# A graph-attention kernel: two more blocks of x through the main loop, and another order of the drain

## The chip, the cores and the metric

The kernel runs on one core of one Trainium2 chip. The metric is the time of one execution on the device in microseconds; of several executions the median is taken. The core has a matrix engine (TensorE, PE in the profile, its weight loads PEld), VectorE (DVE), ScalarE (ACT), GpSimd (POOL), and SyncE (SP), which here only issues DMAs. Sixteen DMA engines carry all transfers.

## The reference, cut to what matters

```python
# x (4096, 512), adj (4096, 4096), W (512, 4*512), a (4, 1024, 1), all float32
ht  = (x @ W).reshape(N, 4, 512).transpose(1, 0, 2)         # four heads
src = einsum('hnd,hd->hn', ht, a[:, :512, 0])
dst = einsum('hnd,hd->hn', ht, a[:, 512:, 0])
e   = leaky_relu(src[:, :, None] + dst[:, None, :], 0.01) + adj[None]
att = softmax(e, axis=-1)
x   = layernorm(x + einsum('hij,hjd->hid', att, ht).mean(axis=0))
```

The entries of adj are 0 or random numbers up to 1e9, and are added to the scores. Where the largest entry of a row leads the second by more than the scores can differ, the softmax is 1 in that column and 0 elsewhere, and the row's result is the layer norm of x[row] + x[col] @ mean of the heads of W.

## The kernel before

`leading_rows` computes that short form for all rows and counts the rows where the lead is too small; `general` would do the whole softmax for blocks that have such rows, behind a branch on the count, and does not run with these inputs. The 4096 rows make NB = 32 blocks of 128; partition p of block ib is row 32 p + ib, so several blocks of x next to each other are one longer run per partition.

For one block the steps are these. VectorE takes maxima of the 64 segments of 64 columns (`segment_maxima`), then the largest segment and its index (`find_segment`). GpSimd gathers that segment of each row from adj in HBM (`lead`, by an indirect DMA). VectorE finds the place in it, and GpSimd gathers the rows x[col] (`find_column`, tile `y`). PE transposes y and ScalarE copies it out of PSUM (`turn`, tile `yt`). `products` multiplies it, in four steps of 128 columns, with the mean of the heads of W (`w_sum`), and `residual` adds the block's x to the same sum by a product with the identity. ScalarE makes the statistics from the sum (`stats`), GpSimd the root (`rstd`), ScalarE the normalised block (`finish`), into the tile `hold`, in which x lay. `row_norm` makes the sums of squares of x for the test.

The main loop runs over t from 0 to 31; in step t the block t is searched, block t − 2 gathers (`COLUMN`), t − 3 is multiplied (`PROJECT`), t − 4 has its statistics (`STATS`) and each second step a pair t − 6 and t − 5 is finished (`FINISH`). The order of all work on each engine is the order of the program text (`manual_schedule`).

All loads and stores of adj, x and out stand on one queue, SP's, in the order of the text. A block of adj is 2 MB; it is loaded whole, or in four pieces of 512 KB for block 0 and the last four (`LATE` = 28 and on), five blocks ahead (`AHEAD`). The x of blocks 0 to 23 comes between the blocks of adj, four blocks at a time (`x_at`). The last eight blocks (`BEHIND` = 24 and on) have their x loaded behind all of adj, two blocks at a time, in step 31. Blocks 24 to 27 are therefore multiplied without x; ScalarE puts their sum by (`put_by`, line 234), and once x is there GpSimd adds it for 24 to 26 and VectorE for 27 (`add_x`, line 237). Block 28 takes its residual at the head of step 31.

After the loop comes the drain: the stores of the finished blocks are issued, blocks 29, 30 and 31 are gathered, transposed and multiplied, the leftover blocks normalised, the bound for the test made (`bound`, in parts), the test and its count done (`test`, `count`, `report`), and the last stores issued. Blocks 28 to 31 and 27 have their statistics and normalisation from VectorE (`moments`, `factor`, `normalise`) with the root on ScalarE; block 31 is multiplied and normalised in two halves. Block 31's column is searched in the whole row of adj (`find_column_in_row`, line 201) rather than in a gathered segment.

Of the kernel before, what the change touches and what calls it, by code (L numbers as in the profile page):

```python
# [9 lines left out]
F32 = mybir.dt.float32  # L10
# [10 lines left out]
P = 128  # L21
# [45 lines left out]
def leading_rows(ctx, tc, x, adj, W, a, out, ident, v, n_bad, any_bad):  # L67
# [15 lines left out]
    LATE = NB - Q  # L83
    BEHIND = LATE - Q

# [126 lines left out]
    def residual(ib):  # L212
        o_ps[ib] = psum.tile([P, D], F32, name="o")
        nc.tensor.matmul(o_ps[ib], ident, hold[:, ib, :], start=True, stop=False)  # L214

# [140 lines left out]
    def bound(part):  # L356

        if part == 0:
            xm = once.tile([P, 1], F32, name="xm")
            nc.vector.tensor_reduce(xm, xx, axis=AX.X, op=OP.max)  # L360
            px = of_bound[0] = psum.tile([1, P], F32, name="px", bufs=1)
            nc.tensor.transpose(px, xm, ident)
        elif part == 1:
            nc.vector.tensor_reduce(xg, of_bound[0], axis=AX.X, op=OP.max)
            nc.scalar.activation(xg, xg, AF.Sqrt)
            pb = of_bound[1] = psum.tile([P, 1], F32, name="px", bufs=1)
            nc.tensor.matmul(pb, ones[0:1, :], xg, start=True, stop=True)
        else:
            nc.vector.tensor_mul(lead_by, of_bound[1], vn)
            nc.vector.tensor_scalar(lead_by, lead_by, 1.05, 110.0, op0=OP.mult, op1=OP.add)  # L370
# [23 lines left out]

    x_at = {lo - 1: (lo, Q) for lo in range(Q, BEHIND, Q)}
    vectors = [(kb, h) for kb in range(KB) for h in range(H)]
# [3 lines left out]
    for t in range(NB):  # L400
# [13 lines left out]
        if t == NB - 1:  # L414
            for ib in (BEHIND, LATE, BEHIND + 2, LATE + 2):
                load_x(ib, 2)
            row_norm(BEHIND)
            row_norm(BEHIND + 1)
            add_x(nc.gpsimd, BEHIND)
        find_segment(t)  # L420
# [11 lines left out]
        if ib >= 0:  # L432
            turn(ib)
            if ib > BEHIND:
                products(ib - 1, KB - 1, KB)
            if ib < BEHIND or ib == LATE:
                residual(ib)
# [12 lines left out]

    row_norm(BEHIND + 2)
    row_norm(BEHIND + 3)
    row_norm(LATE)
    store(nc.sync, 0, Q)
    for ib in range(Q, BEHIND, 2):
        store(nc.sync, ib, 2)
    find_column(NB - 2)
    add_x(nc.gpsimd, BEHIND + 1)
    find_column_in_row(NB - 1)
    add_x(nc.gpsimd, BEHIND + 2)  # L460
    turn(NB - 3)
    products(NB - 4, KB - 1, KB)
    residual(NB - 3)
    products(NB - 3)
    for ib in range(LATE + 1, NB):
        row_norm(ib)
    stats(BEHIND)
    moments(LATE)
    bound(0)
    for ib in range(BEHIND, NB):  # L470
        find_inner(ib)
    factor(LATE)
    normalise(LATE, o_ps.pop(LATE))
    turn(NB - 2)
    residual_in_halves(NB - 1)
    products(NB - 2, 0, 1)
    bound(1)
    add_x(nc.vector, LATE - 1)
    stats(BEHIND + 1)
    moments(LATE - 1)  # L480
    products(NB - 2, 1, KB - 1)
    rstd(slice(BEHIND, BEHIND + 2))
    stats(BEHIND + 2)
    bound(2)
    test()
    pg = count()
    rstd(slice(BEHIND + 2, BEHIND + 3))
    moments(NB - 3)
    factor(LATE - 1, shift=True)
    report(pg)  # L490
    factor(NB - 3)
    normalise(NB - 3, o_ps.pop(NB - 3))
    turn(NB - 1)
    finish(BEHIND)
# [9 lines left out]
    normalise(NB - 2, o_ps.pop(NB - 2))  # L504
    finish(BEHIND + 2)
    finish(BEHIND + 3)
    stats_of_half(NB - 1, 1)
    moments(NB - 1)
    factor(NB - 1, shift=True)
    finish_in_halves(NB - 1)  # L510
    for ib, n in ((NB - 4, 1), (NB - 3, 1), (BEHIND, 2), (NB - 2, 1), (BEHIND + 2, 2)):
        store(nc.sync, ib, n)
# [154 lines left out]
```

## Time and profile before

| | |
|---|---|
| median of 6 runs | 242.54 us (242.29 to 243.21) |
| the profiled execution | 242.08 us, span 240.5 us |
| busy: PE, DVE, ACT, POOL | 83%, 78%, 46%, 42% of the span |
| DMA | 97.73 MB, mean 406 GB/s |
| adj on the SP queue | 27 transfers of 2 MB, 20 of 512 KB |
| x on the SP queue | 6 of 1 MB, 4 of 512 KB |
| stores | 1 of 1 MB, 12 of 512 KB, 4 of 256 KB |

Times in the profile are from the start of the span; the span leaves some 1.6 us of the execution's time outside. In a row of the timeline stand the start, the time taken, the engine, the line, the operation with its tiles and shapes, how many instructions are taken together, and in brackets the engine's idle time before and what ended it. A tile is named as in the program (`seg<-adj_t`: written and read). A 128x512 product in float32 shows as two instructions, so four steps of `products` are eight. The DMA share is the mean busy share of the sixteen engines; it can pass 1 slightly, as packets overlap.

### The profile page before, as it was taken

How to read it: one execution, taken by the hardware profiler on the slowest of the kernel's cores; microseconds unless marked ns; L12 is line 12 of the kernel's file. 1: busy time of each engine (PE TensorE's matmuls, PEld its weight loads, DVE VectorE, ACT ScalarE, POOL GpSimd, SP SyncE). 2: the span in 40 equal slices, each digit the busy share in tenths (PEclk: the TensorE clock that was granted, in tenths of full speed). 3: DMA queues.
4: the chain of work that ended last, by engine and by line, in shares of the span. 5: the costliest groups of instructions: out<-in, count | busy, mean ns of one | idle time of the engine just before them, and what ended most of it. 6: DMA issues, size and time to landing. Idle time of an engine off the chain costs nothing.

```text
span 240.5 us, 2519 instructions
## 1 busy us (share of the span) xinstructions
PE 199.5 (83%) x683; PEld 102.6 (43%) x683; DVE 187.0 (78%) x308; ACT 111.8 (46%) x267; POOL 101.3 (42%) x215
## 2 busy tenths in 40 slices
PE   0198959999999899999959978599878869698990
PEld 0135515656666566655424433143433423243560
DVE  2635784489869985999589969987799999897781
ACT  2002002155757566564635554446464645156771
POOL 1102322316426452646352753454365565567210
PEclk9999778999999999999997999979999999999998
DMA  6999999999999999999999999999999999999995
GB/s 241 440 417 422 420 431 406 425 422 405 424 426 419 403 424 422 415 411 431 403 428 422 411 420 419 418 410 418 415 424 399 399 400 405 396 411 416 418 401 217
DMA packets 14849, 97.73 MB, mean 406 GB/s; under 512 B 2280, under 2 KB 2280, under 8 KB 9968
## 3 DMA queue, kind: packets, MB, share of 16 engines
q1 hardware_dynamic: 11232, 88.09, 89.0%
q0 software_dynamic: 3584, 9.44, 10.1%
q8 instruction: 6, 0.10, 0.2%
q14 instruction: 11, 0.09, 0.1%
q10 hardware_dynamic: 16, 0.02, 0.0%
HBM read 89.15 MB, written 8.39 MB: 405 GB/s over the span
## 4 chain that ended last, share of the span: by engine, by line
issue 34%; POOL 30%; DMA 22%; PE 7%; DVE 3%; ACT 1%; POOLq 1%; SPq 1%
DMA adj_t<-in_adj_dram 15%; POOL lead L171 10%; POOL y L181 9%; DMA y<-in_x_dram,col 7%; PE o L221 3%; POOL sd L249 3%; POOL start L176 2%; POOL col L195 2%; POOL row L169 2%; DVE seg L158 2%; PE o L263 1%; PE tp L208 1%; POOL sd L248 1%; POOL nm L250 1%; SPq L113 1%
## 5 line engine op out<-in xcount | busy, mean ns | idle before, releaser
L158 DVE TENSOR_REDUCE seg<-adj_t 128x32 f32<-128x2048 f32 (+1 forms) x74 | 146.3, 1987 | 38.9 <-DMA adj_t<-in_adj_dram 38.1
L221 PE MATMUL o<-w_sum,yt 128*128 128x512 f32 x248 | 116.5, 610 | 0.7 <-ACT yt L210 0.7
L221 PEld LDWEIGHTS o<-w_sum,yt 128*128 128x128 f32 x248 | 45.5, 194 | 54.5 <-issue 44.1
L210 ACT COPY yt<-tp 128x512 f32<-128x512 f32 x32 | 18.8, 587 | 46.6 <-PE tp L208 46.6
L171 POOL DMA_INDIRECT lead<-in_adj_dram,row x32 | 32.3, 1010 | 14.1 <-POOL row L169 14.1
L181 POOL DMA_INDIRECT y<-in_x_dram,col x32 | 30.9, 965 | 16.1 <-POOL col L195 15.1
L311 PE MATMUL o<-hold,ident 128*128 128x512 f32 x32 | 21.0, 818 | 14.9 <-DMA hold<-in_L_gnn_W_dram 14.9
L208 PE MATMUL tp<-ident,y 128*128 128x128 f32 x128 | 20.0, 280 | 15.4 <-DMA y<-in_x_dram,col 15.3
L214 PE MATMUL o<-hold,ident 128*128 128x512 f32 x52 | 28.0, 620 | 0.2 <-DMA hold<-in_x_dram 0.2
L208 PEld LDWEIGHTS tp<-ident,y 128*128 128x128 f32 x128 | 14.4, 142 | 28.7 <-issue 27.0
L195 POOL TENSOR_TENSOR col<-start,within 128x1 uint32<-128x1 uint32 x31 | 5.9, 190 | 48.7 <-DVE within L193 48.6
L329 ACT COPY wt<-tp 128x512 f32<-128x512 f32 x16 | 9.2, 587 | 31.5 <-PE tp L327 26.9
L169 POOL TENSOR_TENSOR row<-at,first 128x1 uint32<-128x1 uint32 x32 | 6.1, 190 | 38.6 <-DVE at L167 38.6
L228 ACT ACTIVATE sq<-hold 128x512 f32<-128x512 f32 x32 | 19.8, 619 | 2.9 <-DMA hold<-in_x_dram 2.9
L335 PEld LDWEIGHTS pv<-at_d,wt 128*128 128x128 f32 x128 | 16.3, 191 | 6.8 <-ACT wt L329 3.5
L311 PEld LDWEIGHTS o<-hold,ident 128*128 128x128 f32 x32 | 8.1, 264 | 25.4 <-POOL row L169 10.9
L312 ACT ACTIVATE w_sum<-o 128x512 f32<-128x512 f32 x4 | 2.4, 598 | 33.4 <-PE o L311 33.4
L254 ACT ACTIVATE hold<-o,nm,sd 128x512 f32<-128x512 f32 x24 | 17.2, 771 | 0.0
L245 ACT ACTIVATE sq<-o,nm 128x512 f32<-128x512 f32 x24 | 16.5, 688 | 0.8
L335 PE MATMUL pv<-at_d,wt 128*128 128x2 f32 x128 | 15.3, 244 | 0.6 <-ACT wt L329 0.6
L243 ACT ACTIVATE sq<-o 128x512 f32<-128x512 f32 x24 | 14.6, 608 | 0.0
L327 PEld LDWEIGHTS tp<-ident,hold 128*128 128x128 f32 x64 | 7.9, 142 | 6.9 <-issue 6.9
(85 smaller groups left out, 137.6 us busy)
## 6 DMA issues: line engine op xcount, KB each, us to landing
adj_t<-in_adj_dram SPq DMA_DIRECT2D x27, 2048.0 KB
adj_t<-in_adj_dram SPq DMA_DIRECT2D x20, 512.0 KB
hold<-in_x_dram SPq DMA_DIRECT2D x6, 1024.0 KB
out_dram<-hold SPq DMA_DIRECT2D x12, 512.0 KB
hold<-in_L_gnn_W_dram SPq DMA_DIRECT2D x4, 1024.0 KB
hold<-in_x_dram SPq DMA_DIRECT2D x4, 512.0 KB
out_dram<-hold SPq DMA_DIRECT2D x1, 1024.0 KB
out_dram<-hold SPq DMA_DIRECT2D x4, 256.0 KB
```

The source lines that it names most:

```text
L158: nc.vector.tensor_reduce(seg_of[ib][:, ts(k, S // n)], adj_t[ib][:, ts(k, N // n)].rearrange("p (s e) -> p s e", e=E), axis=AX.X, op=OP.max,)
L171: nc.gpsimd.indirect_dma_start(out=lead, out_offset=None, in_=adj_segs, in_offset=bass.IndirectOffsetOnAxis(ap=row[:, :1], axis=0),)
L181: nc.gpsimd.indirect_dma_start(out=y, out_offset=None, in_=x, in_offset=bass.IndirectOffsetOnAxis(ap=col[:, :1], axis=0),)
L208: nc.tensor.transpose(tp[:, kb, :], y[:, ts(kb, P)], ident)
L210: nc.scalar.copy(yt, tp)
L214: nc.tensor.matmul(o_ps[ib], ident, hold[:, ib, :], start=True, stop=False)
L221: nc.tensor.matmul(o_ps[ib], yt_of[ib][:, kb, :], w_sum[:, kb, :], start=(start and kb == 0), stop=(kb == KB - 1),)
L228: nc.scalar.activation(sq, hold[:, ib, :], AF.Square, accum_out=xx[:, ib : ib + 1])
L245: nc.scalar.activation(sq, o, AF.Square, bias=nm[:, i], accum_out=sd[:, i])
L254: nc.scalar.activation(hold[:, ib, :], o_ps.pop(ib), AF.Identity, bias=nm[:, i], scale=sd[:, i])
L311: nc.tensor.matmul(o, ident, hold[:, w_at + kb * H + h, :], start=(h == 0), stop=(h == H - 1))
L335: nc.tensor.matmul(pv[:, kb, h : 2 * H : H], wt[:, k, :], at_d[:, k, h : 2 * H : H], start=(k == 0), stop=(k == KB - 1),)
```

## The change

`BEHIND` goes from 24 to 26. The x of blocks 24 and 25 is one more load between the blocks of adj, issued in step 23 ahead of adj block 28, so the loads behind adj become three (blocks 28 and 29, then 26 and 27, then 30 and 31) instead of four. Blocks 24 and 25 then go the loop's usual way, with residual on PE, statistics in steps 28 and 29 and finish in step 30; only 26 and 27 are put by, and GpSimd adds x for 26 and VectorE for 27. Block 28 is multiplied in step 31 without its residual, which comes after the loop with its last product. In the drain the sums of squares, the inner maxima, the parts of the bound (four now), the test's count and `turn` of block 31 stand elsewhere, block 27's and 29's moments are apart, and a pair fewer is finished.

```diff
-    BEHIND = LATE - Q
+    BEHIND = LATE - 2
     def residual(ib):
-        o_ps[ib] = psum.tile([P, D], F32, name="o")
-        nc.tensor.matmul(o_ps[ib], ident, hold[:, ib, :], start=True, stop=False)
+        start = ib not in o_ps
+        if start:
+            o_ps[ib] = psum.tile([P, D], F32, name="o")
+        nc.tensor.matmul(o_ps[ib], ident, hold[:, ib, :], start=start, stop=False)
 ...
             nc.scalar.activation(xg, xg, AF.Sqrt)
-            pb = of_bound[1] = psum.tile([P, 1], F32, name="px", bufs=1)
+        elif part == 2:
+            pb = of_bound[2] = psum.tile([P, 1], F32, name="px", bufs=1)
             nc.tensor.matmul(pb, ones[0:1, :], xg, start=True, stop=True)
 ...
-    x_at = {lo - 1: (lo, Q) for lo in range(Q, BEHIND, Q)}
+    x_at = {lo - 1: (lo, min(Q, BEHIND - lo)) for lo in range(Q, BEHIND, Q)}
 ...
         if t == NB - 1:
-            for ib in (BEHIND, LATE, BEHIND + 2, LATE + 2):
+            for ib in (LATE, BEHIND, LATE + 2):
                 load_x(ib, 2)
-            row_norm(BEHIND)
-            row_norm(BEHIND + 1)
-            add_x(nc.gpsimd, BEHIND)
 ...
-            if ib < BEHIND or ib == LATE:
+            if ib < BEHIND:
                 residual(ib)
 ...
-    row_norm(BEHIND + 2)
-    row_norm(BEHIND + 3)
-    row_norm(LATE)
+    for ib in range(BEHIND, LATE + 2):
+        row_norm(ib)
     store(nc.sync, 0, Q)
     for ib in range(Q, BEHIND, 2):
         store(nc.sync, ib, 2)
     find_column(NB - 2)
-    add_x(nc.gpsimd, BEHIND + 1)
+    add_x(nc.gpsimd, BEHIND)
     find_column_in_row(NB - 1)
-    add_x(nc.gpsimd, BEHIND + 2)
+    residual(LATE)
+    products(LATE, KB - 1, KB)
     turn(NB - 3)
-    products(NB - 4, KB - 1, KB)
     residual(NB - 3)
-    products(NB - 3)
-    for ib in range(LATE + 1, NB):
-        row_norm(ib)
-    stats(BEHIND)
+    products(NB - 3, 0, KB - 1)
+    row_norm(NB - 2)
+    row_norm(NB - 1)
     moments(LATE)
-    bound(0)
     for ib in range(BEHIND, NB):
         find_inner(ib)
+    bound(0)
+    products(NB - 3, KB - 1, KB)
+    stats(BEHIND)
     factor(LATE)
     normalise(LATE, o_ps.pop(LATE))
+    bound(1)
     turn(NB - 2)
     residual_in_halves(NB - 1)
-    products(NB - 2, 0, 1)
-    bound(1)
+    bound(2)
     add_x(nc.vector, LATE - 1)
-    stats(BEHIND + 1)
     moments(LATE - 1)
-    products(NB - 2, 1, KB - 1)
-    rstd(slice(BEHIND, BEHIND + 2))
-    stats(BEHIND + 2)
-    bound(2)
+    products(NB - 2, 0, 2)
+    bound(3)
     test()
     pg = count()
-    rstd(slice(BEHIND + 2, BEHIND + 3))
+    products(NB - 2, 2, KB - 1)
+    rstd(slice(BEHIND, BEHIND + 1))
+    report(pg)
+    turn(NB - 1)
     moments(NB - 3)
     factor(LATE - 1, shift=True)
-    report(pg)
     factor(NB - 3)
     normalise(NB - 3, o_ps.pop(NB - 3))
-    turn(NB - 1)
     finish(BEHIND)
     finish(BEHIND + 1)
 ...
-    finish(BEHIND + 2)
-    finish(BEHIND + 3)
 ...
-    for ib, n in ((NB - 4, 1), (NB - 3, 1), (BEHIND, 2), (NB - 2, 1), (BEHIND + 2, 2)):
+    for ib, n in ((NB - 4, 1), (NB - 3, 1), (BEHIND, 2), (NB - 2, 1)):
         store(nc.sync, ib, n)
```

More of the change, by code (lines that the diff above doesn't have):

```diff
@@ L365, in bound @@
             nc.scalar.activation(xg, xg, AF.Sqrt)
-            pb = of_bound[1] = psum.tile([P, 1], F32, name="px", bufs=1)
+        elif part == 2:
+            pb = of_bound[2] = psum.tile([P, 1], F32, name="px", bufs=1)
             nc.tensor.matmul(pb, ones[0:1, :], xg, start=True, stop=True)
         else:
-            nc.vector.tensor_mul(lead_by, of_bound[1], vn)
+            nc.vector.tensor_mul(lead_by, of_bound[2], vn)
             nc.vector.tensor_scalar(lead_by, lead_by, 1.05, 110.0, op0=OP.mult, op1=OP.add)
```

## The prediction

> **What bounds the kernel now.** I read the page's slices first. The DMA row says that the sixteen DMA engines are full from the second slice to the last but one, while PE is not.
>
> ```profile
> PE   0198959999999899999959978599878869698990
> DVE  2635784489869985999589969987799999897781
> DMA  6999999999999999999999999999999999999995
> ...
> HBM read 89.15 MB, written 8.39 MB: 405 GB/s over the span
> ```
>
> 97.5 MB at the 415 or so GB/s of the middle slices is 235 us of a 240.5 us span: the kernel moves bytes, and computing matters only where it leaves an engine of the DMA without work. So the second view is the table by windows over the last microseconds (columns: window, its length, busy time of PE, PEld, DVE, ACT and POOL, granted clock, DMA share, GB/s).
>
> ```profile
> 236.25:236.50 0.25, 0.00 (x0) 0.00 (x0) 0.00 (x0) 0.00 (x0) 0.00 (x0) 1.00 0.74 295
> ...
> 236.75:237.00 0.25, 0.00 (x0) 0.00 (x0) 0.00 (x0) 0.00 (x0) 0.00 (x0) 1.00 0.59 238
> 237.00:237.25 0.25, 0.00 (x0) 0.00 (x0) 0.00 (x0) 0.00 (x0) 0.00 (x0) 1.00 1.03 401
> ...
> 238.00:238.25 0.25, 0.00 (x0) 0.00 (x0) 0.00 (x0) 0.00 (x0) 0.00 (x0) 1.00 0.28 115
> ...
> 238.75:239.00 0.25, 0.00 (x0) 0.00 (x0) 0.00 (x0) 0.00 (x0) 0.00 (x0) 0.50 0.17 66
> ```
>
> The second figure from the right is the one to read. The last store (block 31, 256 KB) is issued at 236.16. Before it, between 236.25 and 237.0, a quarter to two fifths of the engines have nothing to do; at 237.0 it reaches them and all are busy. But the last to end, at 239.0, are two or three of sixteen (0.17). 256 KB is 16 KB for each engine, 0.63 us at 415/16 = 26 GB/s; an engine that ends at 239.0 began that store only at about 238.35, 1.35 us after it had reached the idle ones. Those late engines were not waiting for it: they had older stores to finish. This decides the forecast.
>
> The third view is the SP queue in its single issues, with what each waited for, beside the reduces of VectorE.
>
> ```profile
> 211.39 0.33 SPq L306 DMA_DIRECT2D out_dram<-hold  x1
> SPq L306 <- DMA adj_t<-in_adj_dram: 1.4, 1, 1.4
> ...
> 212.85 0.33 SPq L306 DMA_DIRECT2D out_dram<-hold  x1
> SPq L306 <- DMA hold<-in_x_dram: 1.1, 1, 1.1
> ...
> 210.48 3.45 DVE L158 TENSOR_REDUCE seg<-adj_t 128x16 f32<-128x1024 f32 x3
> ```
>
> After the last adj piece (issued 198.95) come four loads of x and then the stores. The four x loads and the first four stores wait for pieces of adj, the next four stores for the x loads: a transfer is issued when the eighth before it has landed. So the issue times tell landings: block 30's four pieces at 200.27, 202.27, 203.50 and 204.95, block 31's at 206.94, 208.17, 209.60 and 211.39, the first x load at 212.85. VectorE takes the pieces of block 31 at 208.49, 210.48, 211.63 and 212.78 (3.45 us is three of 1.15): it is 0.7 to 1.6 us behind the stream there.
>
> Last, the tail, from the timeline of PE and DVE.
>
> ```profile
> 219.09 1.02 PE L221 MATMUL o<-w_sum,yt 128*128 128x512 f32 x2
> ...
> 232.94 0.55 DVE L290 TENSOR_SCALAR hold<-hold,mv,sd 128x512 f32<-128x512 f32 x1
> ...
> 234.14 0.43 DVE L297 BATCH_NORM_STATS2 halves_st<-o 128x6 f32<-128x256 f32 x1 [0.65 <-PE o L263]
> ```
>
> From block 29's transposes (218.62, when its y has landed) PE works nearly without a pause to 234.11. The first row is block 28's last product, behind them; the last is block 31's second half of statistics, for which VectorE waited 0.65 us on PE. Root, normalise and the last store follow.
>
> **The change part by part.**
>
> *x of blocks 24 and 25 (512 KB) moves ahead of the sixteen pieces of blocks 28 to 31.* Bytes, number and size of transfers stay as they were, the stores too (one of 1 MB, twelve of 512 KB, four of 256 KB before and after), so each DMA engine has the same work. Each piece takes the place of the transfer after it: block 30 lands at 202.27, 203.50, 204.95 and 206.94 against uses at 203.14, 204.46, 205.61 and 206.76; block 31 at 208.17, 209.60, 211.39 and 212.85 against 208.49, 210.48, 211.63 and 212.78. Two are late, by 0.18 and 0.07. VectorE has 0.58 us of waiting for the lead gather just before 210.27, which swallows the first. Cost: 0.1 us. Without that cover, if VectorE kept up with the stream, it would be the whole place, 1.4 us. In steps 24 to 27 x comes long before its use. The other x loads land where they did (block 28 about 214.1, blocks 26 and 27 about 215.5).
>
> *Blocks 24 and 25 in the loop.* PE gets two residuals of 0.86 us (two passes of 0.43) in steps 27 and 28. It waited for y 1.47 us before block 25's transposes (197.51), 0.54 before block 26's and 1.88 before block 27's (208.22): covered; without that each would cost 0.86. ACT gets statistics and square sums there (0.60 + 0.69 + 0.62 plus reads, some 2.1 us per block) and loses two copies of 0.59; its gaps before the next yt copy are 3.0, 1.9 and 4.6 us: covered. POOL gets the three rstd operations (1.2 us) in step 30, between y of block 28 (ends 206.57) and the row of block 30, which comes at 208.66: covered. POOL loses two additions of 1.27 us; the one in step 31 held block 31's row by 0.25 us, the other ended before y of block 31, which VectorE's search of a whole row (215.13 to 219.55) releases. So the gathers of y stand as they were, but for 0.2 us at block 30. The finish of both blocks goes to step 30, and their store becomes the twelfth on SP, ahead of block 28's, waiting for nothing but the queue.
>
> *The drain's order on PE.* Block 28 needs its residual no more at the head of step 31, where PE and PEld waited 0.2 and 1.0 us for x, and ACT's yt copy comes 1 us earlier without the two square sums ahead of it. From 212.43: transposes 0.63, block 27's last product 0.86, three of block 28 2.58, residual and last product 1.72, end at 218.2, before y of block 29 lands at 218.5. So 0.86 us leaves the stretch behind 218.62, which PE then ends at 233.25 instead of 234.11. VectorE follows only in part: the root for block 29 now stands on ACT behind the copy of block 31 (228.2 transposes, 228.9 copy, 229.5 root, 229.9 normalise, as now 229.94), so its chain up to the normalise of block 30 still ends at 232.94 + 0.55 = 233.49, and only then comes the second half of block 31. That is 234.14 − 233.49 = 0.65 us gained; bounds 0 (a count or root that waits longer; the test's matmul now stands between products) and 0.86 (VectorE as quick as PE). The last store leaves SP at 235.5.
>
> *What this is worth at the end.* Bounds: 0.65 us if the last store is what ends last, 0 if the loaded engines do. The trace is nearest to 0: the engines that ended at 239.0 had work until 238.35. An issue reaches free engines about 0.85 us later (236.16 to 237.0), so the last store could come as late as 237.5 without moving the end. I take 0.2 us, for small gaps in the late engines' queues that a store waiting earlier would fill. [...]
>
> Sum: 0.2 us off the profiled run's 242.08, that is 241.9; this run was 0.46 under the median 242.54, so 242.3.
>
> **The rivals.**
>
> *Faster: the late engines are late by accident.* Most engines end at 238.2, two or three at 239.0. If their lag (0.75 us) is not there in the new program, the earlier store counts too: −0.65 to −0.95, 241.6 to 241.9. For it: something must have set these few back, and code loading uses the same engines (two instruction queues, 17 packets; six of them take 0.2% of 16 × 240.5 us, 1.3 us each), so its place can move. Against: the code is nearly as long.
>
> *Slower, by the DMA: one such load more, or one on an engine already late.* Place: the last 12 us. Price: 1.3 − 0.2 = +1.1 us, or about half if it falls on an engine less late, 243.0 to 243.6. It decides once an engine with no spare time gets it in the drain. Against: as above.
>
> *Slower, by the stream: adj late on VectorE.* All pieces of blocks 30 and 31 now land within 0.1 to 1.0 us of their use. If the place costs its full 1.4 us, the last store goes at 236.9: still before 237.5, so no change. From a delay of 2.0 us it counts one to one; 2.5 us gives 243.0. Little speaks for that.
>
> *No effect to measure:* this is the forecast itself.
>
> **How the numbers follow.** Forecast, within 0.2% (0.49 us, about what a measurement can tell from no change): 0.53, its own range 242.1 to 242.7. Late engines gone: 0.27. One load more: 0.13; the stream: 0.07. So faster 0.27, same 0.53, slower 0.20. The range leaves one in ten on either side: 241.6 (the faster rival's far end) to 243.1 (into the slower rivals).
>
> **What would show it.** Right: VectorE's last reduce of block 31 still at 212.8 to 212.9; last product of block 28 ahead of block 29's transposes; last store issued about 235.5; DMA share 1.0 from 224 to 234, and a few engines (share 0.1 to 0.2) still working about 238.8. Wrong: the share falls to zero everywhere at once (the store was the bound, faster); the last store after 237.5, or late engines still working after 239.5 (slower).

## The result, and the profile after

The changed kernel is slower: 243.50 us (median of 24 executions, 242.59 to 244.88) against 242.52 us (48 executions, 242.03 to 244.01), a ratio of 1.0039 with a 95% interval of 1.0027 to 1.0051. The forecast was 242.3 us and a range up to 243.1. The executions of the changed kernel spread more: half of them lie between 242.6 and 243.4, half between 243.6 and 244.9, while only two of the 48 of before lie above 243.5. So there are two things to explain: the lower half is some 0.35 us above before's median, and the upper half much more.

The profiled execution of the changed kernel took 242.87 us (span 241.2), 0.79 more than that of before. Its DMA row is as full as before's, but for the end:

```profile
DMA  6999999999999999999999999999999999999994
...
q8 instruction: 6, 0.10, 0.2%
q14 instruction: 11, 0.09, 0.1%
...
HBM read 89.15 MB, written 8.39 MB: 404 GB/s over the span
```

Bytes, packets and code loads (the two instruction queues, 17 packets) are the same in number. What is new stands in the timeline of PE, around the blocks that the drain begins with:

```profile
207.61 3.68 PE L223 MATMUL o<-w_sum,yt 128*128 128x512 f32 x8
213.83 0.63 PE L208 MATMUL tp<-ident,y 128*128 128x128 f32 x4 [2.54 <-DMA y<-in_x_dram,col]
214.30 5.30 PE L223 MATMUL o<-w_sum,yt 128*128 128x512 f32 x8
219.43 1.02 PE L216 MATMUL o<-hold,ident 128*128 128x512 f32 x2
...
221.15 0.60 PE L208 MATMUL tp<-ident,y 128*128 128x128 f32 x4
```

PE has nothing to do for 2.54 us before block 28's transposes, since y of block 28 has not landed; before, these followed at 212.43 without a pause. Then eight product instructions take 5.30 us, where they took 3.68 us at 207.61. The windows say why (columns as in the prediction, granted clock third from the right):

```profile
214.00:216.00 2.00, 2.00 (x7) 1.11 (x7) 0.79 (x4) 0.91 (x2) 0.48 (x2) 0.72 1.03 412
216.00:218.00 2.00, 2.00 (x4) 0.67 (x3) 1.91 (x4) 2.00 (x7) 1.71 (x4) 0.50 1.03 426
218.00:220.00 2.00, 2.00 (x6) 1.04 (x5) 2.00 (x1) 0.72 (x4) 1.54 (x2) 0.93 1.01 416
```

After the pause the clock is halved: 0.56 + 1.0 + 0.14 us are lost in the three windows, which is a stretch of 3.4 us at 0.5 (from 214.87 to 218.28). Before, it was 1.0 there. And why y was late stands in the DMA view of the window from 210 to 213 us (packets, MB, share of the sixteen engines):

```profile
q8 instruction: 1, 0.02, 2.2%
```

One packet of q8, a code load of 16 KB, held one DMA engine for 1.06 us (2.2% of 16 × 3 us) from 211.0 on. The part of y on that engine landed at 213.70, the last of the others at 212.42. In the profile of before the same load (the fifth of the six of 16 KB) came at 205.9, and it was y of block 27 that was late.

Block 29's transposes so start at 221.15 instead of 218.62, and the stores of the drain wait for them, on SP:

```profile
225.74 0.33 SPq L308 DMA_DIRECT2D out_dram<-hold  x1
233.29 0.33 SPq L308 DMA_DIRECT2D out_dram<-hold  x1
...
235.94 0.33 SPq L308 DMA_DIRECT2D out_dram<-hold  x1
237.85 0.33 SPq L308 DMA_DIRECT2D out_dram<-hold  x1
```

The queue gets nothing between 225.74 and 233.29 (before: 230.78), and runs dry; the last store leaves at 237.85 instead of 236.16. The end, in windows:

```profile
232.00:234.00 2.00, 2.00 (x10) 1.72 (x10) 1.68 (x4) 1.62 (x4) 0.00 (x0) 1.00 0.89 354
234.00:236.00 2.00, 1.80 (x9) 1.24 (x7) 1.89 (x6) 0.29 (x1) 0.00 (x0) 1.00 0.66 243
236.00:238.00 2.00, 0.00 (x0) 0.00 (x0) 1.25 (x5) 0.86 (x2) 0.00 (x0) 1.00 0.90 353
238.00:239.00 1.00, 0.00 (x0) 0.00 (x0) 0.00 (x0) 0.00 (x0) 0.00 (x0) 0.88 0.34 129
239.00:240.00 1.00, 0.00 (x0) 0.00 (x0) 0.00 (x0) 0.00 (x0) 0.00 (x0) 0.50 0.46 162
```

A third of the engines' time between 234 and 236 is empty (share 0.66; 0.97 before). Yet the last landing, 240.28, is only 0.69 us later than before's 239.59, though the last store left 1.69 us later.

### The profile page after: what moved, and what is told of

It is laid out like the page before. It is cut to its first block, busy times and chain, and to the rows that moved or that the text cites. A ratio compares the mean times of both kernels' runs of the same rounds, so it can differ in the third digit from the quotient of the medians.

```text
span 241.2 us, 2516 instructions
## 1 busy us (share of the span) xinstructions
PE 201.9 (84%) x687; PEld 103.6 (43%) x687; DVE 187.3 (78%) x308; ACT 110.3 (46%) x265; POOL 99.3 (41%) x213
## 4 chain that ended last, share of the span: by engine, by line
issue 31%; POOL 30%; DMA 17%; PE 16%; ACT 2%; DVE 1%; POOLq 1%; SPq 0%
DMA hold<-in_L_gnn_W_dram 11%; POOL lead L171 10%; POOL y L181 9%; PE o L223 8%; POOL sd L251 4%; DMA y<-in_x_dram,col 3%; PE o L313 3%; DMA adj_t<-in_adj_dram 2%; POOL start L176 2%; POOL col L195 2%; POOL row L169 2%; PE pv L337 1%; PE o L216 1%; PE tp L208 1%; POOL sd L250 1%
## 5 line engine op out<-in xcount | busy, mean ns | idle before, releaser
L223 PE MATMUL o<-w_sum,yt 128*128 128x512 f32 x248 | 117.9, 617 | 0.7 <-ACT yt L210 0.7
L313 PE MATMUL o<-hold,ident 128*128 128x512 f32 x32 | 22.3, 862 | 15.6 <-DMA hold<-in_L_gnn_W_dram 15.6
L216 PE MATMUL o<-hold,ident 128*128 128x512 f32 x56 | 28.9, 598 | 0.0
L256 ACT ACTIVATE hold<-o,nm,sd 128x512 f32<-128x512 f32 x26 | 18.7, 771 | 0.0
L247 ACT ACTIVATE sq<-o,nm 128x512 f32<-128x512 f32 x26 | 17.9, 688 | 0.8
L245 ACT ACTIVATE sq<-o 128x512 f32<-128x512 f32 x26 | 15.8, 608 | 0.0
L251 POOL TENSOR_TENSOR sd<-sd,power 128x2 f32<-128x2 f32 (+1 forms) x14 | 10.5, 753 | 1.2
```

Of the source, the lines that this page charges most:

```text
L216: nc.tensor.matmul(o_ps[ib], ident, hold[:, ib, :], start=start, stop=False)
L223: nc.tensor.matmul(o_ps[ib], yt_of[ib][:, kb, :], w_sum[:, kb, :], start=(start and kb == 0), stop=(kb == KB - 1),)
L251: nc.gpsimd.tensor_tensor(sd[:, i], sd[:, i], power[:, : i.stop - i.start], op=OP.pow)
L256: nc.scalar.activation(hold[:, ib, :], o_ps.pop(ib), AF.Identity, bias=nm[:, i], scale=sd[:, i])
L313: nc.tensor.matmul(o, ident, hold[:, w_at + kb * H + h, :], start=(h == 0), stop=(h == H - 1))
```

## The experiments

Three explanations offer themselves after this profile. The first: the pause and the halved clock make the loss. The second: they cost little, as some DMA engines end late anyway (in the profile of before the last one landed at 239.59, the last but two at 238.63), and the loss comes with the slow engines themselves and the code loaded onto them. The third: it is only the place at which code is loaded, which the change has moved (that load from 205.9 to 211.0). (The expectations number their theories anew. In the first four, theory 1 is this pause, theory 2 the stream, that is x ahead of adj, and theory 3 the drain's order.) All comparisons are with the kernel before on the same chip (medians 242.42 to 242.54).

| kernel | median, us (executions) | ratio to before |
|---|---|---|
| changed, PE kept busy (e1) | 243.28 (8) | 1.0031 [1.0018, 1.0044] |
| x and blocks 24, 25 alone (e2) | 243.02 (11) | 1.0019 [1.0010, 1.0027] |
| drain's order alone (e3) | 242.99 (12) | 1.0016 [0.9998, 1.0035] |
| changed, 84 small instructions and a 16-byte tile (e4) | 241.14 (6) | 0.9944 [0.9931, 0.9957] |
| changed, the same without the tile (e5) | 243.03 (12) | 1.0023 [1.0009, 1.0037] |
| before, the same without the tile (e6) | 242.54 (12) | 0.9999 [0.9988, 1.0011] |
| changed, 32-byte tile (e7) | 241.16 (9) | 0.9950 [0.9932, 0.9969] |
| before, 32-byte tile (e8) | 240.50 (6) | 0.9919 [0.9895, 0.9942] |
| changed, PE busy and block 29's root first (e12) | 242.95 (12) | 1.0020 [0.9998, 1.0043] |
| before, no branch (e13) | 242.26 (11) | 0.9991 [0.9982, 1.0000] |
| changed, no branch (e14) | 242.38 (11) | 0.9992 [0.9982, 1.0003] |
| before, tile ahead of all (e15) | 240.81 (5) | 0.9923 [0.9910, 0.9936] |
| changed, tile ahead of all (e16) | 241.53 (6) | 0.9952 [0.9937, 0.9967] |

**Closing the pause.** Four products with the identity, whose result nobody reads, stand ahead of block 28's transposes.

```diff
+    def keep_busy(n):
+        warm = psum.tile([P, D // 2], F32, name="px", bufs=1)
+        for _ in range(n):
+            nc.tensor.matmul(warm, ident, w_sum[:, 0, : D // 2], start=True, stop=True)
...
+            if ib == LATE:
+                keep_busy(4)
             turn(ib)
```

> The changed kernel, with four more 128x256 products by the identity (1.7 us by the 0.43 us that two passes of such a product took) on PE in step 31, between block 27's third product and block 28's transposes. Their result is read by nobody. Theory 1, the pause: in the changed kernel's profile PE stands 2.54 us before block 28's transposes, and from 214.9 the granted clock is halved for 3.4 us, which puts all that follows 1.7 us behind; with PE kept busy the clock stays 1.0 in 214 to 220, block 29's transposes start about 219.2 instead of 221.15 and the time falls by 0.6 to 1.0 us, to 242.5 to 242.9. Theory 2, the stream: x ahead of adj makes VectorE's search of block 31's row late (216.4 against 215.1), and that costs the time; then 243.5 stays. Theory 3, the drain's order: block 29's normalise behind the copy of block 31 starves the store queue; then 243.5 stays or is worse.

PE's timeline in this kernel:

```profile
211.21 1.89 PE L106 MATMUL px<-w_sum,ident 128*128 128x256 f32 x8
213.87 0.63 PE L213 MATMUL tp<-ident,y 128*128 128x128 f32 x4 [0.77 <-DMA y<-in_x_dram,col]
214.34 3.68 PE L228 MATMUL o<-w_sum,yt 128*128 128x512 f32 x8
...
219.57 0.60 PE L213 MATMUL tp<-ident,y 128*128 128x128 f32 x4
```

y is as late as it was (213.87), but with 0.77 us of pause the clock stays at 1.0, block 29 starts 1.58 us earlier, and the last store leaves at 236.28, as in the kernel before. The time falls by 0.2 us only, and the intervals of the two ratios overlap, so even that isn't certain. Two executions of eight are above 243.5 instead of half of them. The other 0.75 us are still there, and the windows of the end show where:

```profile
238.50:239.00 0.50, 0.00 (x0) 0.00 (x0) 0.00 (x0) 0.00 (x0) 0.00 (x0) 0.50 0.09 37
239.00:239.50 0.50, 0.00 (x0) 0.00 (x0) 0.00 (x0) 0.00 (x0) 0.00 (x0) 0.50 0.08 12
239.50:240.00 0.50, 0.00 (x0) 0.00 (x0) 0.00 (x0) 0.00 (x0) 0.00 (x0) 0.50 0.05 20
```

A share of 0.05 to 0.09 is one engine of sixteen. Fifteen have landed by 239.27; that one lands at 240.45. So the first explanation covers about a fifth, if anything, and perhaps part of the spread.

**The halves of the change.** First the loads and blocks 24 and 25 in the loop, with the drain in before's order, then the drain's order with eight blocks of x still behind adj.

```diff
-    BEHIND = LATE - Q
+    BEHIND = LATE - 2
...
-            for ib in (BEHIND, LATE, BEHIND + 2, LATE + 2):
+            for ib in (LATE, BEHIND, LATE + 2):
...
-    for ib, n in ((NB - 4, 1), (NB - 3, 1), (BEHIND, 2), (NB - 2, 1), (BEHIND + 2, 2)):
+    for ib, n in ((NB - 4, 1), (NB - 3, 1), (NB - 2, 1), (BEHIND, 2)):
```

> One part of the change alone: x of blocks 24 and 25 ahead of block 28's pieces and both blocks in the loop, with the drain in the order of before (block 28's residual at the head of step 31, its last product behind block 29's transposes). Theory 1 (pause before block 28 and half clock): PE comes as early to block 28's y as in the changed kernel, so the pause is there too where y is late; 243.0 to 243.8. Theory 2 (stream): 243.5. Theory 3 (order): 242.5 as before.

```diff
-            if ib < BEHIND or ib == LATE:
+            if ib < BEHIND:
                 residual(ib)
...
+    residual(LATE)
+    products(LATE, KB - 1, KB)
     turn(NB - 3)
-    products(NB - 4, KB - 1, KB)
     residual(NB - 3)
-    products(NB - 3)
+    products(NB - 3, 0, KB - 1)
...
```

> The other part alone: all eight blocks' x behind adj as before, but the drain in the new order (block 28's residual and last product ahead of block 29's transposes, the bound in four parts, the test's count between block 30's products, block 31's transposes ahead of block 29's normalise). Theory 1: no longer pause than before ahead of block 28, the clock stays 1.0; the last store about 0.3 to 0.6 us earlier and the time 242.2 to 242.6. Theory 2: 242.5. Theory 3: 243.5.

Each half costs 0.5 us, and together they make the 1.0 of the whole (the interval of the second just reaches no change). Neither ends with its last store: it left at 237.6 and 236.86, and the last engine landed at 240.42 and 240.84. In both profiles a code load fell at 216.3 to 216.5, and it was y of block 29 that was late. e2's profile has no pause before block 28 (transposes at 213.03), on which its first theory stood, and e3's median lies between the 242.6 and the 243.5 that its theories gave. So no one line carries the loss.

**The place of the code.** 24 tiny instructions each on VectorE, GpSimd and ScalarE and 12 on PE at the start are to move the later code loads.

```diff
+    pad = once.tile([P, 4], F32, name="pad")
+    for _ in range(24):
+        nc.vector.memset(pad[:, 0:1], 0.0)
+        nc.gpsimd.memset(pad[:, 1:2], 0.0)
+        nc.scalar.copy(pad[:, 2:3], eps)
+    for _ in range(12):
+        nc.tensor.matmul(warm[:, 0, :], ident, ident[:, : 2 * H], start=True, stop=True)
```

> The changed kernel with 24 small instructions more on VectorE, on GpSimd and on ScalarE and 12 on PE in the first microseconds, while the engines wait for the first adj; nothing else differs. It moves the places at which blocks of code are loaded: in the changed kernel a 16 KB code load runs on a DMA engine at 211.0, in the middle of the gather of y for block 28, which is complete at 213.7, one engine 1.3 us after the others (before: the load at 205.9, in the gather for block 27). Theory 1 with the code load as the cause of the late y: the load is elsewhere, block 28's transposes start at 212.5, PE's pause is under 1.5 us, the clock stays 1.0, and the time is 242.4 to 242.8. Theory 1 without the code load: pause and time stay, 243.5. Theories 2 and 3: 243.5.

At 241.14 this is 2.4 us faster than the changed kernel, and 1.4 faster than before. That was not the code: `pad` moved every later tile by 32 bytes, and without it the gain is gone (243.03, e5). The same instructions writing to tiles that exist already give the next two rows, after and before:

```diff
+    for _ in range(24):
+        nc.vector.memset(sd[:, 0:1], 0.0)
+    for _ in range(24):
+        nc.gpsimd.memset(nm[:, 0:1], 0.0)
+    for _ in range(24):
+        nc.scalar.copy(xx[:, 0:1], eps)
+    spare = psum.tile([P, KB, 2 * H], F32, name="px", bufs=1)
+    for _ in range(12):
+        nc.tensor.matmul(spare[:, 0, :], ident, ident[:, : 2 * H], start=True, stop=True)
```

> The changed kernel with 24 small instructions more on VectorE, GpSimd and ScalarE and 12 on PE in the first microseconds, as in e4_shift, but written into tiles that are there already, so that no tile lies at another address (in e4_shift a new tile of 16 bytes moved all tiles behind it by 32 bytes, and its 16 KB packets of adj took 613 ns instead of 619). Theory A, the places of the code loads make the second of the change's loss: without the load in the gather for block 28 the time is 242.3 to 242.9. Theory B, they play no part and e4_shift won by its addresses alone: 243.3 to 243.7. Theory C, the drain's order and the stream: 243.3 to 243.7 too.

> The kernel before with the same small instructions. Theory A: the load leaves 205.9, where it was in the gather for block 27, and lands elsewhere: the time can move by up to 1 us either way, 241.8 to 243.5. Theories B and C: 242.5 within 0.2%.

Now the load that fell at 211.0 in the changed kernel falls at 195.3 (e5), and in the kernel before it falls at 211.0 instead of 205.9 (e6). They have changed places, and so has the pause. The kernel before with it:

```profile
214.12 0.63 PE L218 MATMUL tp<-ident,y 128*128 128x128 f32 x4 [2.71 <-DMA y<-in_x_dram,col]
...
216.30 2.74 PE L231 MATMUL o<-w_sum,yt 128*128 128x512 f32 x6
218.88 0.60 PE L218 MATMUL tp<-ident,y 128*128 128x128 f32 x4
```

Its y of block 28 is as late as the changed kernel's, the pause is longer still (2.71 us, though this time the clock stays full), and it costs the median nothing: block 29 starts at 218.88, 0.26 later than before. In its order 4.76 us lie between block 28's transposes and block 29's; in the changed order 5.70 us (213.87 to 219.57 in the rows of e1), since block 28's last product has come ahead of block 29. The changed kernel (e5), with its pause shortened to 1.49 us and a full clock, is still 0.5 us slower. So the place of this one load is not the whole of it: the old order has the pause without loss, and the changed order has a loss without the long pause. Whether the other 0.5 us of the 1.0 belong to this load can't be told, as the intervals of e5 and of the changed kernel overlap.

**Addresses.** An unused tile of 32 bytes per partition ahead of `top`, in both kernels.

```diff
+    once.tile([P, 8], F32, name="room")
     top = once.tile([P, NB, 8], F32, name="top")
```

> The changed kernel with an unused tile of 32 bytes ahead of the tile of segment maxima, so that the tiles of adj lie 32 bytes further (at a multiple of 64 bytes), and no instruction more. Theory of the addresses: 16 KB packets take 613 instead of 619 ns; 216 of them and 288 of 4 KB on each engine give 1.2 to 1.4 us, so 243.5 becomes 242.1 to 242.3. If it was the code's place alone that helped e4_shift: 243.5 stays.

> The kernel before with the same unused tile of 32 bytes. Theory of the addresses: 242.5 becomes 241.1 to 241.3, ahead of both kernels. Otherwise 242.5.

Both gain about 2 us, more than the 1.2 to 1.4 that was expected, and most of the distance stays: 241.16 to 240.50, 0.66 us. The kernel before with this tile is the fastest of all, 0.8% under both kernels of the case. These two profiles are also the cleanest test of the forecast, as neither has a halved clock around block 28: the last store leaves at 235.60 in the old order and at 234.91 in the new one, 0.69 us earlier (forecast 0.65). And then, in the new order:

```profile
237.00:237.50 0.50, 0.00 (x0) 0.00 (x0) 0.00 (x0) 0.00 (x0) 0.00 (x0) 0.50 0.12 45
237.50:238.00 0.50, 0.00 (x0) 0.00 (x0) 0.00 (x0) 0.00 (x0) 0.00 (x0) 0.50 0.08 29
238.00:238.50 0.50, 0.00 (x0) 0.00 (x0) 0.00 (x0) 0.00 (x0) 0.00 (x0) 0.50 0.06 8
238.50:239.00 0.50, 0.00 (x0) 0.00 (x0) 0.00 (x0) 0.00 (x0) 0.00 (x0) 0.50 0.05 20
```

and in the old one:

```profile
236.50:237.00 0.50, 0.00 (x0) 0.00 (x0) 0.00 (x0) 0.00 (x0) 0.00 (x0) 0.50 1.03 389
237.00:237.50 0.50, 0.00 (x0) 0.00 (x0) 0.00 (x0) 0.00 (x0) 0.00 (x0) 0.50 0.42 148
237.50:238.00 0.50, 0.00 (x0) 0.00 (x0) 0.00 (x0) 0.00 (x0) 0.00 (x0) 0.50 0.00 0
```

In the new order fourteen engines have ended by 237.10, one at 237.95, and one works on; the last landing is at 239.43, against 238.02 in the old order. What was gained by the earlier store is gained on fourteen engines and lost on one.

With the tile ahead of all others, so that x, y, the gathered segments and adj all move together, the change costs the same again, +0.7 us, and the kernel before gains nothing over e8 (240.81 against 240.50):

```diff
     any_bad = keep.tile([1, 1], I32, name="any_bad")
+    keep.tile([P, 8], F32, name="room")
```

> The kernel before with an unused tile of 32 bytes ahead of all big tiles, so that x, y, the segments and adj lie at multiples of 64 bytes (in e8_before_room adj, y and the segments did, x did not). If addresses at odd multiples of 32 bytes cost each packet 1%: 88 MB of adj and x gain what 78 MB of adj did and some 0.2 us more, 240.2 to 240.5; if only adj's matters, 240.5.

> The changed kernel with the same unused tile. If the change costs the same at these addresses: 0.4 to 1.0 us behind e15, 240.8 to 241.4. If its loss came from the places that landings happened to have against the pieces' use, it is another here, and can be none.

Here both profiles have the pause (2.63 and 2.65 us) and the half clock, the one of the old order too, and the change still costs what it did. The last stores leave at almost the same time, 235.98 and 236.13, and the last engine lands at 238.38 in the old order and at 239.37 in the new one. So here the pause isn't what parts the two kernels.

**The same kernels again**, unchanged: a second profile of the kernel before, a second and a third of the changed one.

> The kernel before once more, for a second profile. If what the first one showed belongs to the kernel, PE again has no pause over 1.1 us behind 209 and the slowest DMA engine ends within 1.0 us behind the others; 242.1 to 242.7. If it belongs to the execution, a pause or a lag of the changed kernel's size is seen here too.

> The changed kernel once more, for a second profile. If the pause and the half clock belong to the kernel: block 28's transposes again behind a pause of 2 us or more, and the last store about 237.8; 242.8 to 244.5. If they belong to the execution: no half clock behind 209, the last store near 236, and the slowest DMA engine decides.

> The changed kernel a third time, with the same expectation as for its second profile: with three one can tell what comes back. Its 24 earlier times spread from 242.6 to 244.9, so I expect at least one of the three without the half clock.

The kernel before took 242.29 us, without a pause before block 28. The changed kernel, second profile (243.07 us):

```profile
209.27 0.63 PE L208 MATMUL tp<-ident,y 128*128 128x128 f32 x4 [1.81 <-DMA y<-in_x_dram,col]
...
213.25 0.60 PE L208 MATMUL tp<-ident,y 128*128 128x128 f32 x4
213.69 3.68 PE L223 MATMUL o<-w_sum,yt 128*128 128x512 f32 x8
...
219.57 0.63 PE L208 MATMUL tp<-ident,y 128*128 128x128 f32 x4 [0.48 <-DMA y<-in_x_dram,col]
```

and third profile (244.28 us):

```profile
215.24 0.76 PE L208 MATMUL tp<-ident,y 128*128 128x128 f32 x4 [2.60 <-DMA y<-in_x_dram,col]
215.79 5.21 PE L223 MATMUL o<-w_sum,yt 128*128 128x512 f32 x8
```

So it is a matter of the execution: the same program had that load at 206.8 once (block 27 waits 1.81 us, at full clock) and at 211.0 and 212.1 in the other two (block 28 waits 2.5 to 2.6 us and the clock is halved). In the third profile the last store left at 239.26 and landed at 241.68. That is an execution of the upper half of the spread; the 242.87 us of the first profile, with pause and half clock too, is not. The second has no pause there and is still 0.6 us above before's median: its last store left at 236.30, as before's, and one engine landed at 240.46.

**An earlier root.** In the changed order, block 29's statistics and root stand behind block 31's transposes. Put ahead of them, on top of the busy PE:

```diff
...
     rstd(slice(BEHIND, BEHIND + 1))
-    report(pg)
-    turn(NB - 1)
     moments(NB - 3)
     factor(LATE - 1, shift=True)
+    report(pg)
     factor(NB - 3)
     normalise(NB - 3, o_ps.pop(NB - 3))
+    turn(NB - 1)
```

> The changed kernel with PE kept busy before block 28 as in e1_busy, and with block 29's moments, root and normalise ahead of block 31's transposes as in the kernel before, so that their root no longer stands behind block 31's copy on ScalarE. Theory of the order: block 29's store leaves at about 230 instead of 231.7, the last store before 236, the DMA engines get no gap, and the time falls from the 243.3 of e1_busy to 242.5 to 242.8. Theory of the slow engine: the last store is not what ends last, and 243.2 to 243.4 stays.

Block 29's store leaves at 229.85 instead of 231.71, so the queue doesn't run dry, and the last one at 236.14; one engine still lands at 240.28. The last store's time is then before's, and 0.5 us is still lost in the median (the interval just reaches no change).

**Without the branch.** What remains is the one slow engine. Code is loaded at the very end too, behind the last store's issue, where the program branches on the count: two loads of 8 KB on the queue q14, at 238.08 and 238.95 us in the profile of before, 0.31 us each. In the DMA view from 236 to 242 us they stand so, for the kernel before:

```profile
q14 instruction: 2, 0.02, 0.6%
```

and for the changed kernel in its second profile:

```profile
q14 instruction: 2, 0.02, 1.0%
```

That is 0.6 and 1.0 us of engine time for the two loads together (of 16 × 6 us); the first profile of the changed kernel has 0.6% too. These two kernels (e13, e14) leave out the read of the count, the branch and the general code behind it, which doesn't run.

```diff
-    flag = nc.values_load(any_bad[0:1, 0:1], min_val=0, max_val=N)
-    with tc.If(flag > 0, preferred_fallthrough_block=True, label="general"):
-        general(tc, x, adj, W, out, ident, v, n_bad)
...
-        if t == NB // 2:
-            tc.mark_branch_hint_location("general", engines=HINTED)
```

> The kernel before without the read of the count, the branch and the general part behind it (it does not run with these inputs), and without the hint for that branch. It is the partner of e14. On every theory it is some 0.5 to 1.5 us faster than before, as the engines no longer read the flag after the last store is issued.

> The changed kernel without the read of the count, the branch, the general part and the hint. Theory of the code loads at the end: no instruction is loaded behind the last store's issue, the slow DMA engine loses 0.5 us less, and what is left against e13 is what the pause and half clock cost, 0.0 to 0.4 us in the median, with the fastest runs of both equal. Theory that the order or the stream costs it: e14 stays 0.7 to 1.0 us behind e13, fastest runs too.

Here the change costs 0.1 us, and nothing that can be measured: 242.38 to 242.26. The kernel before gains 0.2 us from the missing branch (0.5 to 1.5 had been expected on every theory), the changed one 1.1. More than the two loads at the end is gone: neither profile has a code load behind 228, and those with the branch have four behind 231, one of 16 KB and one of 8 KB up to 236 and the two at the end. The profile of the changed one even has the pause and the half clock:

```profile
213.65 0.63 PE L205 MATMUL tp<-ident,y 128*128 128x128 f32 x4 [2.65 <-DMA y<-in_x_dram,col]
214.12 5.29 PE L220 MATMUL o<-w_sum,yt 128*128 128x512 f32 x8
```

but its end is another, although the last store leaves at 237.68, only 0.17 earlier than with the branch:

```profile
238.50:239.00 0.50, 0.00 (x0) 0.00 (x0) 0.00 (x0) 0.00 (x0) 0.00 (x0) 0.50 0.97 369
239.00:239.50 0.50, 0.00 (x0) 0.00 (x0) 0.00 (x0) 0.00 (x0) 0.00 (x0) 0.50 0.42 156
239.50:240.00 0.50, 0.00 (x0) 0.00 (x0) 0.00 (x0) 0.00 (x0) 0.00 (x0) 0.50 0.00 0
```

All engines take the last store together and end together, at 239.69 instead of 240.28.

How the slow engine gets slower can be read from the landings of the last three stores in the trace. The table has how long the last engine is behind the third last, at each:

| profile | last but two | last but one | last |
|---|---|---|---|
| before | 0.77 | 0.77 | 0.96 |
| before, second profile | 0.93 | 0.97 | 1.06 |
| before, small instructions (e6) | 1.15 | 1.12 | 1.44 |
| before, no branch (e13) | 0.72 | 0.73 | 0.73 |
| changed, second profile (e10) | 0.63 | 0.87 | 1.17 |
| changed, PE busy (e1) | 1.02 | 1.14 | 1.71 |
| changed, root first (e12) | 0.99 | 1.25 | 1.54 |
| changed, small instructions (e5) | 0.85 | 1.13 | 1.33 |
| changed, 32-byte tile (e7) | 1.72 | 2.02 | 2.33 |
| changed, 16-byte tile (e4) | 0.89 | 0.92 | 1.32 |
| changed, tile ahead of all (e16) | 0.82 | 0.82 | 1.23 |
| before, 32-byte tile (e8) | 1.06 | 1.00 | 0.28 |
| before, tile ahead of all (e15) | 0.78 | 0.75 | 0.37 |

Over the last two stores the slow engine loses nothing without the branch, and 0.4 to 0.7 us in the new order with it. In the old order with it, it loses 0.1 to 0.3 us, and with the moved tiles (e8, e15) it draws nearer instead. (Not in the table are the profiles of the changed order in which the queue ran dry, after, e11 and e14, where the engines had time to draw level, and the halves e2 and e3. The last store but one is 512 KB in the old order, 256 KB in the new.)

The trace's packets show what the slow engine does there. From the place where the last code load starts (238.69 us in e1, 238.95 in the kernel before) the DMA view to 240.5 has, for e1,

```profile
q1 hardware_dynamic: 11, 0.02, 3.7%
q14 instruction: 1, 0.01, 1.1%
```

and for the kernel before

```profile
q14 instruction: 1, 0.01, 1.2%
q1 hardware_dynamic: 1, 0.00, 0.0%
```

In e1 the load runs from 238.70 to 239.00, right behind the engine's part of the last store but one, and ahead of its part of the last store. That part, eight packets of 2 KB, follows from 239.00 to 239.98. Its first three packets take 0.126, 0.265 and 0.227 us, where such packets take 0.084 in the median. The load's 0.31 us and 0.37 us for the three slow packets make 0.68; the table has 0.69 in all (1.02 to 1.71). (The trace doesn't name a packet's engine. That the load ran on this one is read from the times: from 238.77 to 239.00 no data packet begins, and the first one begins as the load ends.) e10, e12 and e7 have the same load in the same place, and the same three slow packets to within 0.005 us. In the kernel before the last load comes when the store's data have gone, and delays nothing.

This divides the profiles by the order of the drain. In all six with the old order and the branch (before, e9, e6, e8, e15, e2) no data packet begins once the last code load has ended. With the new order 6 to 15 do (e1, e10, e12, e7, e5, e4, e16 and the drain's order alone, e3), but for the two profiles whose last store was late by the pause (after, e11).

## Why the prediction was wrong

*What bounds the kernel: right.* The end is set by one or two slow DMA engines. With the last store at the same time as before (236.14 to 236.30: e1, e10, e12) the end still moves, by 0.5 to 0.9 us; with the store 0.69 earlier than in e8 (e7) it is later too; with the store 1.69 later (the first profile) only 0.69.

*That a last store up to 237.5 costs nothing: half right.* In e14 a store at 237.68 finds all engines free and the median is before's. But 237.85 in the first profile cost something, and 239.26 in the third took the end to 241.68.

*x of 24 and 25 ahead of adj, 0.1 us: too small.* One reading of the prediction contradicts its own figures: VectorE was not 0.7 to 1.6 us behind the stream at block 31's pieces, but 1.4 to 2.3 (1.55, 2.31, 2.03 and 1.39); the sum doesn't use it. VectorE's last piece of block 31 came later than worked out:

```profile
213.05 1.22 DVE L158 TENSOR_REDUCE seg<-adj_t 128x16 f32<-128x1024 f32 x1 [0.35 <-DMA adj_t<-in_adj_dram]
...
216.09 0.09 DVE L193 MATCH_VALUE_LOAD within<-top,lead 128x8 f32 x1 [1.16 <-DMA lead<-in_adj_dram,row]
...
216.42 4.42 DVE L201 FIND_INDEX8 col<-top,adj_t 128x8 uint32<-128x4096 f32 x1
```

213.05 is 0.27 after the 212.78 of before, and the search of block 31's row starts 1.29 us later, most of it through the wait for a gathered segment. The gather of block 31's y lands at 228.09 and PE is not yet there. With this part alone (e2) the median rises 0.5 us; that profile was also half a microsecond late on the stream, so the two can't be parted.

*Blocks 24 and 25 in the loop, covered: not contradicted.* PE finishes block 27's products at 211.29, earlier than before's 212.41.

*The drain on PE: the lengths right, the start wrong.* The first step that failed is "From 212.43: transposes 0.63, ..., end at 218.2, before y of block 29 lands at 218.5". It took PE's start on block 28 from the profile of before, where it was PE that was late. In the changed kernel PE is ready at 211.3, and y of block 28 became what is waited for. When a 16 KB code load falls on its landing, block 28 starts at 213.83; the 5.7 us of work then reach 219.53, 0.91 past 218.62, and the halved clock adds 1.62 (5.30 − 3.68): 221.15. From there on the steps hold: PE ended its last product at 235.80, 14.65 us after block 29's start, where the prediction had 14.63; the last store, forecast 235.5 plus the delay of 2.53, is 238.0, measured 237.85. In e7, without that pause, the earlier store came as forecast. Two of the three profiles of the changed kernel have pause and half clock. What they cost in the median is 0.2 us by e1, within the noise. One execution of the upper half of the spread was profiled, e11; it has both, but so have the 242.87 us of the first profile and e14's 242.38, so what makes the upper half isn't shown.

Not the length of the pause alone parts the profiles with half clock from those without. With gaps of 2.54 (after), 2.60 (e11), 2.65 (e14), 2.63 (e15) and 2.65 us (e16) came some 3.4 us at 0.5, with gaps of 2.44 (e13) and 2.71 us (e6) none. In the traces of before and after, the changes of the granted clock lie whole multiples of 3.41 us apart (in after at 27.14, 30.55, 33.96, 40.79, 126.12, 129.54, 214.87, 218.28 and 238.76). A grid of that step, laid through each profile's own changes, is an estimate of mine. On it, 2.37 to 2.65 us of the gap lie in one step where half clock came (after, with 211.46 to 213.83, e11, e14, e15, e16). In e6 and e13 the gap is parted, 1.34 + 1.36 and 0.96 + 1.48 us, and 1.90 us in one step (e8) were not enough. That the place on the grid decides is a reading of these eight profiles; no run moved the gap alone.

*What this is worth at the end: the sign of the 0.2 us was wrong.* This is the step that decided the miss. It was "0.2 us, for small gaps in the late engines' queues that a store waiting earlier would fill". There was no such gain. The late engine loses 0.4 to 0.7 us over the last two stores with the new order, instead of 0.3 at most, and without the branch nothing: the term that was missing is the 8 KB load at the branch, with the slow packets behind it 0.68 us on the engine that ends last (e1). This is what the second rival described, a code load on an engine that is late already (243.0 to 243.6, chance 0.13), with two corrections: no load was added, as their number is the same; and it is the two small loads at the branch, whose time I didn't cost. "Against: the code is nearly as long" was an argument on the amount of code, where its place and time count. The price of 1.3 us for a load came from a share rounded to 0.2%; the six took 1.02 to 1.18 us each in the profile of before.

The trace shows code loads of 16 KB (q8) and of 8 KB (q14). One of 16 KB cost time where the DMA engines were full (share 1.04 from 210 to 213 us in after): the part of a gather on its engine landed 1.28 us behind the last of the others (213.70 against 212.42).

*What stays open.* That the loss needs the branch is shown (0.1 us without, 1.0 with), and the packets show one load of the branch costing the last engine 0.68 us in the new order and nothing in the old. No run moved these loads alone: e13 and e14 also lack the read of the count and the two loads between 231 and 236. Why the last load comes ahead of the last store's data in the new order and behind them in the old isn't known, and why the one load falls at 206.8 in one execution and at 211.0 or 212.1 in others neither. Nor can the 1.0 us be divided exactly: the filled pause gives 0.2, the missing branch 1.1, and e14 kept its pause without loss.

## What to carry to other kernels

Where the DMA engines are full to the end, look at the slowest engine of the sixteen, not at when the last store is issued: an earlier store is a gain only on the engines that would have waited for it (in e7 it was issued 0.69 us earlier than in e8; fourteen engines gained by it, and the last one landed 1.41 us later). When an engine is freed of work, ask what it will then wait for, and take that arrival's lateness (here a gather beside a code load, 1.28 us) instead of the old start time. The branch at the end of this kernel loaded code (8 KB, 0.31 us in e1) when the last engine had no time to spare. And one profile shows one placing of the code loads (206.8, 211.0 and 212.1 us in three of the changed kernel): for an effect under half a per cent look at several executions of the same kernel before a wait is blamed.

## What the runs showed of the hardware that had not been expected

*With the tiles of adj 32 bytes further, their DMA packets took 1% less.* In the kernel before a 16 KB packet takes 619 ns in the median of 3456; with the tiles of adj 32 bytes further (e8; by its expectation and e7's at a multiple of 64 bytes) it takes 613 ns. Only these places were compared. Mean times are 624.7 and 619.5 ns, so these packets alone take 1.1 us less of each engine's time; all packets together take 239.0 us per engine in the profile of before and 236.7 with the 32-byte tile (237.3 in e15). The kernel before gains 2.0 us with it (0.9919), the changed one 2.3. The 16-byte tile that e4 declares moved every later one by 32 bytes, which is how e4 misled.

*Three packets behind a code load were slow.* In e1 an 8 KB load took 0.31 us of an engine, and the three packets of 2 KB behind it 0.62 us instead of 0.25. In the profiles without the branch no 2 KB packet behind 236 us took over 0.094 us.

*With a pause of some 2.6 us PE's clock was halved for 3.4 us* in five profiles (2.54 to 2.65 us), but not with 2.44 (e13) and 2.71 us (e6). With a few products ahead that nobody reads the pause was 0.77 us and the clock stayed full (e1). In this kernel, bound by its DMA, this was worth 0.2 us in the median, within the noise.
